# Reordering routing, setup and row gathers around the expert halves of a four-layer attention and mixture-of-experts kernel

## The chip, the core and the metric

The kernel runs on one core of one Trainium2 chip. The metric is the device time of one execution in microseconds. The engines are named as in the profile: PE (TensorE, matrix products), DVE (VectorE), ACT (ScalarE), POOL (GpSimd) and SP (SyncE, which here only issues transfers).

## The reference

Four layers run on `x`, 4 batches of 512 tokens with 128 channels, in float32. Each layer is a cross attention on a context of 154 rows per batch, added to `x`, and then a mixture of 8 experts, added to `x`. Both read a layer norm of `x`.

```python
x = x + _L0_xattn_ref(_layernorm(x), ctx, ...)      # bidirectional attention flow, one similarity
x = x + _L0_ffn_ref(_layernorm(x), ...)             # 8 experts, top 2, gated by silu
x = x + _L1_xattn_ref(ctx, ctx, _layernorm(x), ...) # 16 heads of 8, with a mask
x = x + _L1_ffn_ref(_layernorm(x), ...)             # 8 experts, top 1, capacity 321, gelu
x = x + _L2_xattn_ref(_layernorm(x), ctx, ...)      # 16 heads of 64, gated
x = x + _L2_ffn_ref(_layernorm(x), ...)             # 8 experts, top 2, gelu
x = x + _L3_xattn_ref(_layernorm(x), ctx, ctx, ...) # 16 heads of 64
x = x + _L3_ffn_ref(_layernorm(x), ...)             # 8 experts, top 2, relu
```

The reference computes every expert for every token and weighs the results; only the chosen experts have a weight that isn't zero.

## The kernel before

**Tiles and halves.** A batch is 4 tiles of 128 tokens (`NI`). All of `x` stays on the chip. The mixture is computed in two halves of two batches each: half 0 is batches 0 and 1, half 1 batches 2 and 3.

**Routing (`route`, L651).** A generator in steps: layer norm of the half's two batches (`stats` L218, whose power of -0.5 runs on POOL at L236; `norm` L239), transposes (`transposed` L248), logits (L666), the choice of experts (`top` L626), a rank of every token in its expert by products with a triangular matrix (L693, L695), and from it a row number in a buffer in HBM in which each expert owns whole blocks of 128 rows. One indirect transfer for each tile of 128 tokens and each choice scatters the normed rows there (`scatter` L721). The transfers are not issued at once: they are put in the list `rows_due`, and `row_transfers` (L641) issues the next few of them on POOL's queue, bound behind an instruction that it is given.

**Experts (`experts`, L825).** 23 blocks of 128 rows (15 where each token has one expert), in steps of one block (layer 0) or two. `load` (L835) fetches four blocks of tokens after all the scatters of the half, `tokens` (L846) transposes them (L850), `up` (L855) fetches the block's expert weights and multiplies (L877), and `down` (L882) applies the activation, multiplies with the second matrix (L916), copies the result to `ys` (L925, with `row_transfers` behind it) and stores it to `ybuf` in HBM (L928).

**Gather and combine (L948, L965).** After all stores of a half, each tile of tokens fetches its result rows by one indirect transfer per choice (L953) into `yg`, and DVE adds them with their weights to `x` (L971). `combine` requires that no row transfer is still due.

**Attention.** Layer 0 works on whole batches (`layer0_setup` L974). Layers 1 to 3 run a period for each tile of 128 tokens (`narrow_period` L435, `wide_period` L486), in which one tile's scores and exps (L308) run beside the previous tile's transposes of the probabilities (L371), their copies `pT` (L264, `take` L373, which issues two rows each) and products with the values (L408). The next batch is prepared in four parts, one for each tile (`at.parts`, for layer 1 at L1193). Before layer 1 to 3, batch 0 is prepared during the experts of the layer before, as `at.early` (mask, keys, values) and `at.late` (norm, its transpose, queries).

**Order.** In the attention of layers 1 to 3 the order on PE and ACT (in layers 2 and 3 on DVE too) is that of the program (`manual_schedule` L1305). Elsewhere, and on POOL, SP and layer 1's DVE, a scheduler with a model of times sets the order when the kernel is built: the program's order is the priority, and what it believes ready may go ahead. On the chip each engine then runs its instructions in that fixed order. The main loop (L1356 to L1399) sets the program's order: attention with half 0's routing inside, the next layer's setup, half 0's experts with half 1's routing inside, gather of half 0, early preparation, half 1's experts with the combining of half 0 inside, late preparation; half 1's rows are combined in the next layer's first periods.

## Time and profile before

| What | us |
|---|---|
| Median of 3 runs (1345.8 to 1351.96) | 1347.79 |
| The profiled execution's own time | 1282.47 |
| Its span, first to last instruction | 1280.8 |
| PE busy | 1089.4 |
| DVE busy | 731.6 |
| ACT busy | 565.3 |
| POOL busy | 253.6 |
| DVE waiting for gathered rows at L971, all of the kernel | 59.5 |

The profiled execution was shorter than the three timed runs. Its mean granted TensorE clock was 0.917 of full speed. The stages lie in its span about like this: layer 0's attention and first routing to 103 us, layer 0's experts to 262, layer 1's attention to 480, its experts to 573, layer 2's attention to 800, its experts to 906, layer 3's attention to 1140, its experts to 1251, and the last combining to the end.

A line of the order of time reads: start in us, duration in us, engine, line of the kernel, operation, output and inputs, count, and in brackets the idle time of the engine before it with what ended it. `PEld` is a weight load of TensorE, `issue` a time in which the engine waited for nothing that the profile shows. A line of the waits reads: engine and line that waited, what it waited for, us in total, number of times, longest.

### The profile page before, as it was taken

The page shows a single profiled execution, that of the slowest core. Times are in us where ns is not written, and L with a number is a line of the kernel's source. Part 1 is how long each engine was busy: PE and PEld are TensorE (multiplying, and loading weights), DVE is VectorE, ACT ScalarE, POOL GpSimd, SP SyncE. Part 2 cuts the span into 40 slices and gives each one's busy share as a digit, 9 for nine tenths or more (in the row PEclk, how much of TensorE's full clock was granted, in tenths as well). Part 3 has the DMA queues.
Part 4 walks back from the last instruction along what each step waited for, and adds up shares of the span by engine and source line. Part 5 has one row for each costly group of instructions (what it writes and reads, how often), then busy time and mean ns, then how long its engine had stood idle before and what let it go on. Part 6 is the DMA issues. An engine that isn't in the chain of part 4 may idle for free.

```text
span 1280.8 us, 26318 instructions
## 1 busy us (share of the span) xinstructions
PE 1089.4 (85%) x9351; PEld 896.9 (70%) x9351; DVE 731.6 (57%) x2012; ACT 565.3 (44%) x2264; POOL 253.6 (20%) x281
## 2 busy tenths in 40 slices
PE   4787998977878888889999998966899999899990
PEld 3657998933435448787878777855778788789890
DVE  6554646567666763335665776424476576646352
ACT  2113433454554543546656565321656665532230
POOL 2041315023000010232000004045220000402334
PEclk8767999988898988998999999887999999999996
DMA  7023786721100314433112214444421111334762
GB/s 228 1 81 113 216 253 189 207 94 25 23 19 26 100 38 119 133 110 84 35 35 55 64 37 123 123 150 133 127 55 45 41 35 35 109 95 143 209 191 60
DMA packets 136064, 126.77 MB, mean 99 GB/s; under 512 B 12538, under 2 KB 115583, under 8 KB 135551
## 3 DMA queue, kind: packets, MB, share of 16 engines
q1 hardware_dynamic: 128767, 110.39, 30.5%
q0 software_dynamic: 7168, 14.69, 3.9%
q8 instruction: 77, 1.26, 0.4%
q14 instruction: 52, 0.43, 0.1%
HBM read 101.31 MB, written 23.72 MB: 98 GB/s over the span
## 4 chain that ended last, share of the span: by engine, by line
PE 59%; DVE 12%; DMA 9%; issue 8%; ACT 5%; POOL 5%; SPq 2%; POOLq 0%; DVEq 0%
PE sc L877 11%; PE av L916 6%; PE tr L371 6%; PE sc L607 5%; PE av L408 5%; PE tr L425 5%; PE sc L592 3%; DMA yg<-ybuf,su 3%; POOL yg L953 3%; ACT probs L308 3%; DVE nm L294 3%; PE sc L1175 2%; DMA w<-in_up 2%; PE av L390 2%; PE tr L358 2%
## 5 line engine op out<-in xcount | busy, mean ns | idle before, releaser
L308 ACT ACTIVATE probs<-sc,nm 128x154 f32<-128x154 f32 x768 | 286.9, 403 | 162.7 <-DVE nm L294 162.5
L877 PE MATMUL sc<-tokT,w 128*128 128x128 f32 x1528 | 201.3, 286 | 8.7 <-DMA w<-in_up 3.6
L877 PEld LDWEIGHTS sc<-tokT,w 128*128 128x128 f32 x1528 | 189.0, 200 | 15.5 <-ACT eg L900 5.2
L294 DVE TENSOR_REDUCE nm<-sc 128x6 f32<-128x924 f32 x144 | 142.6, 1007 | 74.8 <-PE sc L607 49.1
L308 ACT ACTIVATION_READ_ACCUMULATOR probs<-sc,nm 128x1 f32 x768 | 168.3, 219 | 0.0
L916 PE MATMUL av<-w,hT 128*128 x1160 | 155.3, 279 | 3.2 <-DVE hT L905 2.5
L953 POOL DMA_INDIRECT yg<-ybuf,su x112 | 106.7, 952 | 246.5 <-ACT pT L267 59.9
L722 POOL DMA_INDIRECT buf<-xn,su x112 | 109.6, 979 | 227.0 <-DVE eb L745 97.3
L916 PEld LDWEIGHTS av<-w,hT 128*128 128x128 f32 x1160 | 141.9, 193 | 8.9 <-issue 4.7
L236 POOL TENSOR_TENSOR rstd<-ve,nhalf 128x4 f32<-128x4 f32 x32 | 33.0, 1032 | 547.3 <-DVE ve L234 429.6
L264 DVE COPY pT<-tr 128x512 f32<-128x512 f32 x160 | 106.9, 684 | 45.3 <-PE tr L371 41.5
L408 PE MATMUL av<-pT,vm 128*64 128x128 f32 (+1 forms) x1536 | 106.2, 284 | 22.5 <-DVE pT L264 22.4
L371 PE MATMUL tr<-ident,probs 128*128 128x128 f32 x768 | 123.1, 291 | 1.5 <-DVE rT L337 1.5
L371 PEld LDWEIGHTS tr<-ident,probs 128*128 128x128 f32 x768 | 86.1, 146 | 33.4 <-issue 21.7
L408 PEld LDWEIGHTS av<-pT,vm 128*64 128x64 f32 (+1 forms) x1536 | 63.8, 126 | 55.7 <-DVE pT L264 30.9
L900 ACT ACTIVATE eg<-sc,w 128x128 f32<-128x128 f32 x184 | 52.9, 368 | 89.5 <-PE sc L877 82.1
L607 PE MATMUL sc<-kT,qT 64*128 64x154 f32 x1024 | 87.1, 308 | 4.8 <-ACT probs L308 4.8
L905 DVE SCALAR_TENSOR_TENSOR hT<-sc,w,eg 128x128 f32<-128x128 f32 x184 | 56.2, 342 | 51.0 <-ACT eg L900 51.0
L607 PEld LDWEIGHTS sc<-kT,qT 64*128 64x128 f32 x1024 | 71.3, 189 | 15.8 <-issue 9.9
L592 PE MATMUL sc<-xnT,wq 128*128 128x128 f32 x512 | 73.6, 303 | 4.7 <-ACT probs L308 2.3
L592 PEld LDWEIGHTS sc<-xnT,wq 128*128 128x128 f32 x512 | 67.3, 212 | 10.2 <-issue 3.6
L425 PE MATMUL tr<-wo,aT 128*128 128x128 f32 x512 | 66.2, 284 | 1.6 <-DVE xnT L256 1.3
(255 smaller groups left out, 1432.2 us busy)
## 6 DMA issues: line engine op xcount, KB each, us to landing
w<-in_up SPq DMA_DIRECT2D x46, 516.0 KB
w<-in_up SPq DMA_DIRECT2D x76, 258.0 KB
rep<-rd SPq DMA_DIRECT2D x64, 256.0 KB
tok<-buf SPq DMA_DIRECT2D x36, 256.0 KB
ybuf<-ys SPq DMA_DIRECT2D x58, 128.0 KB
w<-in_down SPq DMA_DIRECT2D x3, 2048.0 KB
w<-in_up SPq DMA_DIRECT2D x46, 128.0 KB
ybuf<-ys SPq DMA_DIRECT2D x52, 64.0 KB
```

The costliest lines, as they stand in the source:

```text
L264: return nc.vector.tensor_copy(o, i)
L294: nc.vector.tensor_reduce(self.at.heads(self.nm, g, n), self.sc[g][:, :, 0 : n * S2].rearrange("p j (s k) -> p j s k", s=n), AX.X, ALU.max ...
L308: nc.scalar.activation(self.pr[:, h, :], self.sc[g][:, j, s * S2 : (s + 1) * S2], AF.Exp, bias=self.nm[:, h : h + 1], accum_out=self.rs[:, ...
L371: nc.tensor.transpose(q[:, t * P : (t + 1) * P], self.pr[:, h, 0:P], ident)
L408: nc.tensor.matmul(av[rows, cols], v, self.pT[n][:, t, :], start=False, stop=last)
L425: nc.tensor.matmul(o[:, 0:D], self.aT[:, c, :], self.at.wo[:, c, :], start=(c == 0), stop=(c == self.nb - 1))
L592: nc.tensor.matmul(sc[:, c // 4, c % 4 * P : (c % 4 + 1) * P], wq[:, c * P : (c + 1) * P], at.xnT[:, i * P : (i + 1) * P], start=True, sto ...
L607: nc.tensor.matmul(sc[:, j, s * S2 : (s + 1) * S2], at.qT[i][rows, c, :], at.kT[rows, c, :], start=True, stop=True)
L722: ins = nc.gpsimd.indirect_dma_start(out=buf[half], out_offset=bass.IndirectOffsetOnAxis(ap=su[:, t : t + 1], axis=0), in_=xns[t // NI][:, ...
L877: nc.tensor.matmul(dst, w[:, b, at : at + P], xT, start=True, stop=True)
L916: nc.tensor.matmul(y[:, b * D : (b + 1) * D], hT[:, fc, :], w2[:, bass.ds(es[b], 1), fc, :].rearrange("p o d -> p (o d)"), start=(fc == 0) ...
L953: ins = nc.gpsimd.indirect_dma_start(out=yg[:, t, :], out_offset=None, in_=ybuf[half], in_offset=bass.IndirectOffsetOnAxis(ap=su[:, t : t ...
```

## The change

Six things are edited, and the halves get a table `GROUPS` of batches in place of fixed arithmetic (the groups stay as they were, two batches in each half).

1. *Routing of layer 0 by batch.* In layer 0 `route` does norm, transposes and logits of one batch in one step, then of the other. `attend_first` runs batch 0's step before tile 1's attention, batch 1's after it, and the first steps of half 1's routing before and after batch 3's attention.
2. *Setup.* `layer1_setup` is called after half 0's experts of layer 0, no longer before them.
3. *Keys ahead.* Half 1's first token transposes are ordered behind the last product of the early preparation.
4. *Gathers.* `yg` is one tile for each batch and choice. Batch 0's rows are issued at once behind the last store, the rest three or four for each `down`. Combining of half 0 is put after 3 (layer 0) or 2 steps of half 1's experts, where it was after 9, 3, 5 and 5.
5. *Layer 1's first tiles.* Half 1's gathers are issued behind the exps of the very first tile too, and their combining starts one tile earlier.
6. *Layer 1's parts.* The norm moves to the third part, its transpose to the fourth, together with keys and queries. Several small tiles have one buffer instead of two or four.

```diff
         def exp(self, g):
...
-                    nc.scalar.activation(
+                    ins = nc.scalar.activation(
...
+            if self.at.dh < 64 and self.at.first and self.i == 0:
+                row_transfers(3, ins)
...
-            self.tails = p2.tile([self.rows, 4, P], F32, tag="tails", name="tails")
+            self.tails = p2.tile([self.rows, 4, P], F32, tag="tails", name="tails", bufs=1)
...
-        lg = rsm("lg", NH, E)
-        found = [stats(x[2 * half + k]) for k in range(B // 2)]
-        yield
-        xns = [norm(x[2 * half + k], found[k], rt) for k in range(B // 2)]
-        yield
-        xnTs = [transposed(xn) for xn in xns]
-        yield
-        for k, xnT in enumerate(xnTs):
...
+        for some in ([b] for b in batches) if layer == 0 else (batches,):
+            found = [stats(x[b]) for b in some]
+            if layer:
+                yield
+            new = [norm(x[b], f, rt) for b, f in zip(some, found)]
+            if layer:
+                yield
+            xnTs = [transposed(xn) for xn in new]
+            if layer:
+                yield
+            for xnT in xnTs:
+                q = ps_tr()
...
+            yield
...
-                nc.tensor.transpose(q[:, c * P : (c + 1) * P], tok[:, c, :], ident)
+                ins = nc.tensor.transpose(q[:, c * P : (c + 1) * P], tok[:, c, :], ident)
+                if g == 0:
+                    wait_for(ins, ahead, "they fill the wait for the tokens")
...
-                2 * n, nc.vector.tensor_copy(ys[:, 0:n], y[:, 0 : n * D].rearrange("p (b d) -> p b d", b=n))
+                2 + n, nc.vector.tensor_copy(ys[:, 0:n], y[:, 0 : n * D].rearrange("p (b d) -> p b d", b=n))
...
+    class Gathered:
...
+        def __init__(self, choices):
+            self.rows = [p2.tile([P, NI, D], F32, tag="yg", name="yg", bufs=6) for _ in range(choices)]
+            self.begun = 0
...
-        assert not rows_due
-        for (cw, _), yg in zip(routed[1], got):
-            nc.vector.scalar_tensor_tensor(xi, yg[:, t, :], cw[:, t : t + 1], xi, ALU.mult, ALU.add)
+        while got[k].begun < NI * len(routed[1]):
+            row_transfers(1)
+        for (cw, _), yg in zip(routed[1], got[k].rows):
+            nc.vector.scalar_tensor_tensor(xi, yg[:, i, :], cw[:, t : t + 1], xi, ALU.mult, ALU.add)
...
-            at.parts = ((masks,), (xn, values), (xnT,), (keys_queries,))
+            at.parts = ((masks,), (values,), (xn,), (xnT, keys_queries))
...
         tiles = [prepare(b, found[b]) for b in range(2)]
         tiles[0](0)
+        first, second = (Steps(route(layer, half, *gates[layer])) for half in range(2))
         tiles.append(prepare(2, found[2]))
+        first.step(1)
         tiles[1](0)
-        beside = Steps(route(layer, 0, *gates[layer])).step(3)
+        first.step(1)
         tiles.append(prepare(3, found[3]))
-        beside.step(5)
+        first.step(4)
         tiles[2](0)
-        beside.step(1)
+        first.step(1)
+        second.step(1)
         tiles[3](0)
-        return beside.finish()
+        return first.finish(), second.step(1)
...
-                    step = nothing if (b, i) in ((0, 0), (0, 1), (2, 0)) else beside.step
+                    step = nothing if (b, i) in ((0, 0), (2, 0)) or layer > 1 and (b, i) == (0, 1) else beside.step
...
         row_transfers()
-        if layer < 3:
+        if 0 < layer < 3:
             prepare = setups[layer + 1]()
...
         stores = first.finish()
         row_transfers()
-        got = gather(0, routed[0], stores)
+        got = gather(layer, 0, routed[0], stores)
+        row_transfers(NI * TOP[layer])
+        early = ()
         if layer < 3:
+            if layer == 0:
+                prepare = setups[1]()
             at = prepare(0, found)
-            for part in at.early:
-                part()
-        second = Steps(experts(layer, 1, routed[1], w2)).step((9, 3, 5, 5)[layer])
-        for k in range(B // 2):
+            early = [part() for part in at.early][-1:]
+        second = Steps(experts(layer, 1, routed[1], w2, early)).step((3, 2, 2, 2)[layer])
+        for k, b in enumerate(GROUPS[layer][0]):
             for i in range(NI):
-                combine(0, k, i, routed[0], got)
+                combine(layer, 0, k, i, routed[0], got)
```

The values function of each layer now returns its last product, for the third edit. Layer 0's `xn` pool has four buffers instead of three.

## The prediction, as it was put on record

> **What bounds the kernel now.** I read the busy shares first, then who TensorE waited for in each stage, then the order of time around the longest waits.
>
> ```profile
> span 1280.8 us, 26318 instructions
> PE 1089.4 (85%) x9351; PEld 896.9 (70%) x9351; DVE 731.6 (57%) x2012; ACT 565.3 (44%) x2264; POOL 253.6 (20%) x281
> ```
>
> TensorE (PE) is the busiest engine. A scheduling change can only win the time in which it waits, so I list its waits by stage (us in total, times, longest). First the start, 0 to 110 us (layer 0's attention and its first routing):
>
> ```profile
> PE tr L251 <- DVE xn L243: 7.9, 2, 4.4
> PE tr L850 <- DMA tok<-buf: 6.5, 1, 6.5
> PE tr L693 <- DVE sel L687: 5.5, 1, 5.5
> ```
>
> L251 waits for a normed batch, L693 (ranks) for the top-2 choice on VectorE (DVE), L850 for tokens scattered to HBM and read back. Then 805 to 915 us, where layer 2's experts pass from half 0 to half 1 and layer 3 is prepared:
>
> ```profile
> PE tr L850 <- DMA tok<-buf: 11.0, 2, 10.1
> PE tr L251 <- DVE xn L243: 11.0, 2, 10.2
> ```
>
> Two stops of 10 us. GpSimd's (POOL) order of time explains the second:
>
> ```profile
> 854.07 0.96 POOL L722 DMA_INDIRECT buf<-xn,su  x1 [0.30 <-issue]
> 867.16 0.98 POOL L953 DMA_INDIRECT yg<-ybuf,su  x1 [12.12 <-DVE ys L925]
> ...
> 885.98 0.94 POOL L953 DMA_INDIRECT yg<-ybuf,su  x1 [0.30 <-issue]
> 886.94 1.05 POOL L236 TENSOR_TENSOR rstd<-ve,nhalf 128x4 f32<-128x4 f32 x1
> ```
>
> The last scatter ends at 855.0. Then POOL idles 12.12 us, because the first gather is tied to a result copy `ys` of the next half, issues 16 gathers in 20 us, and only then makes batch 0's `rstd`. Its input stood ready much earlier:
>
> ```profile
> 880.97 0.21 DVE L234 TENSOR_SCALAR ve<-mv 128x4 f32<-128x4 f32 x1
> ```
>
> and TensorE, next in its order, stands still until 889.2:
>
> ```profile
> 889.22 0.48 PE L251 MATMUL tr<-ident,xn 128*128 128x128 f32 x1 [10.17 <-DVE xn L243]
> ```
>
> In layer 1's first four attention tiles (262 to 312) PE's waits are
>
> ```profile
> PE av L408 <- DVE pT L264: 6.2, 3, 2.9
> PE tr L358 <- DVE res L1189: 5.3, 2, 4.5
> ```
>
> and DVE's own longest there is for gathered rows:
>
> ```profile
> DVE x L971 <- DMA yg<-ybuf,su: 6.7, 9, 1.6
> ```
>
> The gathers run from 274.1, where POOL starts behind a pT copy, to 300.2, and DVE, which runs in order, stops for them.
>
> **What the Trainium skill says.** (1) Perfetto Trace Analysis, the timeline of the Tensor Engine Instruction: ACT, DVE and GPSIMD are strict FIFO. The trace agrees: `rstd` started at 886.94 though `ve` ended at 881.2, with five gathers between. (2) DMA: Bandwidth & Descriptors, Anatomy of one DMA: about 2.0 us fixed plus bytes/436e3, an estimate of 2.15 us for a 64 KB row transfer. The chain of waits shows 2.4 to 3.7 us for `yg`, up to 5.0 beside layer 3's weight loads; I use 2.5 to 3.6. (3) TensorE: Matmul & The Clock Gate, Part 1: after an idle window of about 3.4 us the array runs at half clock. The trace agrees: sixteen L592 matmuls right after the 10 us stop took 3.78 us, at 925.6 they took 2.05.
>
> **The change part by part** (profiled execution: 1282.47 us, of which 1280.8 are span).
>
> *A. Layer 0's routing by batch, setup moved.* Before, both batches' 16 logit matmuls (2.04 us at 61.15) follow tile 3's similarity matmuls (2.42 at 58.94). After, batch 0's eight are done during tile 1 and batch 1's stand ahead of those: 2.42 + 1.02 = 3.4 us earlier. DVE interleaves other work, so I take -3. The norming wait itself (4.4) stays. Batches 2 and 3 are routed before experts start: 8 transposes (1.04 at 113.9) and 16 logit matmuls (2.04) leave a full PE and go partly into the 6.5 us token wait; batch 3's `xn` ends at 104.4, so evacuation 0.69 and logits 1.0 delay the tokens by some 0.6. Net -2. Layer 1's setup leaves this stage: four transposes (1.1 us) and a 0.5 us wait for `wo_r`, about 2 us of DVE, five small SP loads. It returns at about 190 us, where PE is 95% busy, so only the wait is won. The moved loads have no inputs and may issue whenever SP is free (a layer 2 load landed at 30); if that cover is gone, half 1's tokens wait one landing, about 2 us. **Sum A: -5 (bounds -8 to -1).**
>
> *B. Layer 0, half 0 to half 1.* The first gather is already at 193.8, right at the end of half 0; issuing eight without pacing starts nothing earlier. DVE waits 9.0 us for rows at 195 to 224; combining moves from step 9 to step 3. **0 (-2 to +3).**
>
> *C. Layer 1's attention.* Gathers are tied to the exps of the first tile, so they may start before any pT copy; what is late next is the last store of ybuf, which the chain shows taking 7.12 us from 262.1. So they start at 269.3, not 274.1, and without pauses: 16 x 1.26 = 20 us, the last landing near 291 instead of 302.6. Combining starts one tile earlier too. I return half of DVE's 6.7: -3.4. Against it: `xnT` moves into the part with the query matmul. The matmul now waits for a 0.68 evacuation behind a pT copy of 0.69, less the key matmul 0.43 that covers it: 0.25 to 0.95, I take 0.8, for three batches +2.4; ACT's exps stand behind that query copy. **-1 (-8 to +6).**
>
> *D. Layer 1 to 2.* Four gathers (top 1) start when the stores land, about 534, against 544.4. PE's waits there are 1.11 (L251) and 1.80 (L592, `xnT` in a crowded DVE). **-2 (-4 to +1).**
>
> *E. Layer 2 to 3.* Scatters still end at 855.0; eight gathers follow until 865.1, landing by 867.8; two combines 0.7, stats 0.5, `ve` 0.2: ready at 869. Four gathers of batch 1, tied to the first `ys` (866.5), hold POOL to 871.6; `rstd` 1.0, first norm 0.4: PE can go on at 873.2. The late parts stand after 4 steps instead of 7, where PE arrives at 872 (step 4 at 868.05, then the down product of 870.72). The stop falls from 10.2 to about 1.3, and sixteen L592 run at full clock, -1.7: -10.6. If POOL's order puts the last four gathers ahead too, 5 us return. I take **-8 (-11 to -2).** Stop 1, 10.1 us for tokens, stays.
>
> *F. Contention.* The early gathers (8 x 64 KB) share the DMA engines with the token loads (2.8 to 3.2 us, engines 28% busy there): +0.3 in three layers, **+1 (0 to +2).**
>
> *At nothing:* keys ahead of the token transposes, since in layers 1 and 2 they stand there already (L556 at 528.4 and 844.1, L850 at 535.9 and 859.4); the added wait is PE for PE, and holds only what followed in order. Three scatters a block instead of two, since half 1's scatters end at 164 and its tokens are used from 187. One buffer for `tails`, `eq` and the small tiles, since their reader stands before the next writer on an ordered engine; uncovered it is a wait of 0.6 at a `tails` copy. The tail after 1251 (16 gathers, 20 us) is untouched.
>
> **Sum:** -5 + 0 - 1 - 2 - 8 + 1 = -15, so 1267.5 against 1282.5. The shown runs have a median of 1347.79, 1.051 times the profiled execution. I do not know where that share lies and scale: 1267.5 x 1.051 = **1332**.
>
> **The rivals.**
> *Washed out:* `rstd` stays behind all sixteen gathers (E -2.5), early rows only shift DVE's stops (C +2.5), A -3, D -1, F +1: -3, 1279.5, 1345 scaled. For it: DVE and POOL are fixed orders made beforehand, and DVE already stops nine times in C.
> *Slower:* combining now comes 1 to 6 steps sooner in the second half. If DVE's order puts eight combines ahead of the expert copies, it waits 8 x 1.26 + 2.5 = 12.6 us after the last store in each of the four layers. PE has two blocks of work before it needs a copy (two result buffers), 4.2 to 5.8 us, so it loses 7.6: +30 on my -15, 1297.5, 1364 scaled. It decides from (15 + 6.4)/4 = 5.4 us per layer on. For it: at 200.4 L916 waited 2.5 us for `hT` behind row waits. Against: rows land earlier now, and in layer 2 DVE is idle until tokens come.
> *More:* every part at its good end and the clock kept: -33, 1249.5, 1313 scaled.
> *It doesn't do what it says:* true of the keys alone, which I count at nothing.
>
> **How the numbers follow.** About 0.5% (6.7 us) is what a measurement here can tell. My case (1322 to 1341) 0.52, more 0.20, washed out 0.16, slower 0.12. So faster 0.72, same 0.16, slower 0.12. The range 1314 to 1347 leaves out the slower case and the outermost of the others; the likeliest case's own range is 1322 to 1341.
>
> **What would show it.** E: the first `yg` gather within 1 us of the last scatter, `rstd` 8 or 12 gathers later, L251's wait under 3 us. C: first gather near 269, last near 289, DVE's row wait under 4. A: L693 about 3 us earlier, and logit matmuls inside the token wait near 100. D: L251 and L592 without waits near 555. Wrong if L971's waits grow by more than the stops shrink, or if the token waits grow.

## The result, and the profile after

The changed kernel takes 1370.97 us (median; 1368.2 to 1373.3), the kernel before on the same chip 1349.63: a ratio of 1.016, 95% interval 1.0125 to 1.0195. The forecast was 1332 us, faster by 1.2%; the change is slower by 1.6%.

One fact has to come first, because no number below can be read without it. The prediction's trace of the kernel before spans 1280.8 us, its timed runs took 1346 to 1352, and the prediction scaled by 1.051 without knowing why. The chips are of two kinds. On one kind the kernel before takes 1280 to 1281 us in the median (two groups of runs), on the other 1348 to 1356 (four groups); the trace had been taken on the first, the times on the second. One thing that differs is shown further on: TensorE's signals (the semaphore increments that tell the other engines that a product is done) are held up beside row transfers. So I call them **prompt** and **holding** chips. A trace may only be compared with one of the same kind. The page of the changed kernel's first trace, on a holding chip:

```profile
span 1366.5 us, 26291 instructions
...
PE 1116.8 (82%) x9351; PEld 914.8 (67%) x9351; DVE 731.7 (54%) x2012; ACT 562.8 (41%) x2262; POOL 254.9 (19%) x281
```

and of the kernel before on a holding chip (experiment c1):

```profile
span 1344.9 us, 26318 instructions
...
PE 1112.0 (83%) x9351; PEld 913.4 (68%) x9351; DVE 728.7 (54%) x2012; ACT 563.9 (42%) x2264; POOL 253.6 (19%) x281
```

TensorE's busy time differs by 4.8 us of the 21.6, so it is mostly waiting that grew. To see where, I took marks from the timelines (first and last product of TokenT with the up weights in each half, first and last exp of an attention, last result copy) and the time between them, in us:

| stretch | prompt: before, after | holding: before, after | predicted |
|---|---|---|---|
| start to the first expert product | 108.2, 126.0: **+17.8** | 110.4, 126.8: **+16.4** | A, with the next: -5 |
| layer 0, half 0 | 74.4, 70.9: -3.5 | 75.7, 75.1: -0.6 | |
| layer 0, half 1 | 75.4, 75.3: -0.1 | 77.6, 86.3: **+8.7** | B: 0 |
| layer 1, first to last exp | 216.6, 215.7: -0.9 | 214.6, 217.7: +3.1 | C: -1 |
| layer 1's experts | 95.7, 94.1: -1.6 | 99.2, 95.6: -3.6 | D: -2 |
| layer 2's attention | 223.6, 224.3: +0.7 | 235.0, 237.4: +2.4 | |
| layer 2's experts | 108.6, 99.8: **-8.8** | 122.2, 110.5: **-11.7** | E: -8 |
| layer 3's attention | 230.9, 227.8: -3.1 | 247.5, 249.6: +2.1 | |
| layer 3, half 0 | 67.6, 70.1: +2.5 | 74.7, 74.5: -0.2 | |
| layer 3, half 1 | 46.3, 47.6: +1.3 | 55.7, 61.0: **+5.3** | |

On prompt chips the stretches of B, C, D and E moved about as forecast (C's by luck, as the last part shows), and A's did not. On holding chips two more stretches are lost, both beside gathers that are issued without a pause.

**The start.** TensorE's waits, 0 to 130 us, of the changed kernel on a prompt chip (us in total, times, longest):

```profile
PE tr L260 <- DVE xn L252: 21.6, 5, 5.1
```

L260 is the old L251, where the list of before had 7.9 in 2. One of those, 3.5 us, is the first norm of the kernel in both. The other, 4.4 before, has become four: 4.67, 4.45, 5.14 and 3.9, one for each batch. What one of them is made of stands in the timeline of all engines (start, us, engine, line, operation, and the idle time before it with its releaser):

```profile
89.15 0.39 PE L1119 MATMUL av<-wc,xnT 128*128 128x128 f32 x2
89.58 0.69 DVE L1122 TENSOR_TENSOR res<-av,bqv 128x512 f32<-128x512 f32 x1 [3.76 <-PE av L1119]
90.30 0.69 DVE L1124 TENSOR_TENSOR x<-x,res 128x512 f32<-128x512 f32 x1
...
91.03 0.87 DVE L236 BATCH_NORM_STATS2 st<-x 128x6 f32<-128x128 f32 x4
91.82 0.36 DVE L238 BATCH_NORM_AGGREGATE mv<-st 128x2 f32<-128x6 f32 x4
...
92.21 0.17 DVE L243 TENSOR_SCALAR ve<-mv 128x4 f32<-128x4 f32 x1
93.11 1.04 POOL L245 TENSOR_TENSOR rstd<-ve,nhalf 128x4 f32<-128x4 f32 x1
94.19 1.12 DVE L252 TENSOR_SCALAR xn<-x,mv,rstd 128x128 f32<-128x128 f32 x4 [1.81 <-POOL rstd L245]
94.68 1.15 PE L260 MATMUL tr<-ident,xn 128*128 128x128 f32 x4 [5.14 <-DVE xn L252]
```

A tile's last product ends at 89.5; residual, statistics, GpSimd's rstd (behind a row transfer) and norm follow one another, and TensorE does nothing, because the transposes of just this batch are next in its order. Only then comes the next tile:

```profile
96.62 1.88 PE L687 MATMUL tr<-wg,xnT 128*128 128x8 f32 x8 [0.78 <-DVE xnT L98]
98.35 1.09 PE L1074 MATMUL tr<-ident,sim 128*128 128x128 f32 x4
```

In the kernel before, the next tile's similarity (L1033) stood in the middle of the tile ahead of it:

```profile
33.27 1.20 PE L1078 MATMUL av<-wqv,ft 128*128 128x128 f32 x4
...
34.47 1.06 PE L1033 MATMUL tr<-ident,sim 128*128 128x128 f32 x4
...
61.15 2.04 PE L666 MATMUL tr<-wg,xnT 128*128 128x8 f32 x16
```

The last lines show a second price: the eight logit products of each batch took 1.88 us, sixteen before took 2.04, 0.235 us each against 0.128. The eight at 96.62 begin 1.9 us after their stop ends, the sixteen 3.7 us after theirs (the one of 4.4 us), with other products between. The Trainium skill, TensorE: Matmul & The Clock Gate, Part 1, has the array at half clock after an idle window of about 3.4 us; the trace agrees here, where each of the four stops is longer than that, but a shorter stop, 2.6 us in layer 2 to 3 below, did it too.

**Layer 2 to 3.** GpSimd's order of time on the prompt chip, around the last scatter:

```profile
865.51 0.96 POOL L744 DMA_INDIRECT buf<-xn,su  x1 [0.30 <-issue]
866.77 0.98 POOL L988 DMA_INDIRECT yg<-ybuf,su  x1 [0.30 <-issue]
...
882.75 0.95 POOL L988 DMA_INDIRECT yg<-ybuf,su  x1 [0.30 <-issue]
883.73 1.05 POOL L245 TENSOR_TENSOR rstd<-ve,nhalf 128x4 f32<-128x4 f32 x1
```

The first gather follows the last scatter at once (before: 12.12 us of idling), and rstd comes after 12 gathers instead of 16. TensorE's and VectorE's waits, 815 to 922:

```profile
DVE x L1012 <- DMA yg<-ybuf,su: 15.5, 10, 5.8
...
PE tr L875 <- DMA tok<-buf: 8.8, 1, 8.8
...
PE tr L260 <- DVE xn L252: 3.7, 3, 2.6
```

```profile
886.19 0.33 PE L260 MATMUL tr<-ident,xn 128*128 128x128 f32 x1 [2.59 <-DVE xn L252]
...
889.35 3.62 PE L604 MATMUL sc<-xnT,wq 128*128 128x128 f32 x16
```

The stop of 10.2 us is 2.6; the token wait stays, as predicted. VectorE waits longer for rows than before (9.6 us in 9 there). The sixteen query products behind the stop still take 3.62 us, about as slow as the 3.78 before, so the 1.7 us that E had for them at full clock did not come.

**Held signals.** On the holding chip, layer 0 half 1 has a stop that belongs to no instruction:

```profile
222.86 0.61 PE L943 MATMUL av<-w,hT 128*128 x4
...
228.70 0.95 POOL L988 DMA_INDIRECT yg<-ybuf,su  x1 [0.30 <-issue]
230.89 0.29 DVE L952 COPY ys<-av 128x128 f32<-128x128 f32 x1 [8.78 <-remote]
...
231.49 1.23 PE L943 MATMUL av<-w,hT 128*128 x4 [8.03 <-issue]
```

VectorE's copy waits for a TensorE product that ended at 220.1, and TensorE for what VectorE would do next. The trace also has the times at which TensorE's semaphore was counted up. Nine of its instructions that count it end in this stretch, and nine increments are recorded; set side by side in order:

```
instruction ends  218.34  218.86  219.61  220.08  223.02  223.25  223.47  232.29  232.72
increment         219.47  226.64  229.46  230.87  235.25  235.29  235.33  235.37  235.41
```

The fourth is the end of the product that the copy needs: 230.87, and the copy starts at 230.89. The fifth, 12.2 us late, is the up product that ScalarE needs, and ScalarE goes on at 235.27. So these two pairs are confirmed by the engines that waited; the first three are paired by order alone, and four increments just before them are missing from the record. The last five come in a burst 40 ns apart, 1.6 us after GpSimd's run of gathers ended (233.65). Counting as late an increment that is recorded more than 0.35 us from the end of every instruction making one:

| trace | TensorE late | of these in the 3 us after a row transfer's start | span, us |
|---|---|---|---|
| before, prompt | 2 of 1338 | 0 | 1280.8 |
| after, prompt (c2) | 2 of 1331 | 0 | 1283.7 |
| before, holding (c1) | 109 of 1305 | 98 | 1344.9 |
| after, holding | 89 of 1307 | 70 | 1366.5 |

The stretches of 3 us after a row transfer's start make up 26% of the span in c1 and hold 98 of its 109 late increments. Over all traces the two kinds stand apart: 72 to 109 late increments in each of eleven, 2 in each of nine. ScalarE's and VectorE's increments are not late on either kind (2 of 745 and 2 of 1761 in c1). On holding chips some increments are missing from the record (1305 of 1342 made), so the counts are lower bounds.

### The profile page after: what moved, and what is told of

Read it like the earlier page. It is cut to its first block, busy times and chain, and to the rows that moved or that the text cites. A ratio compares the mean times of both kernels' runs of the same rounds, so it can differ in the third digit from the quotient of the medians.

```text
span 1366.5 us, 26291 instructions
## 1 busy us (share of the span) xinstructions
PE 1116.8 (82%) x9351; PEld 914.8 (67%) x9351; DVE 731.7 (54%) x2012; ACT 562.8 (41%) x2262; POOL 254.9 (19%) x281
## 3 DMA queue, kind: packets, MB, share of 16 engines
q1 hardware_dynamic: 128767, 110.39, 28.6%
## 4 chain that ended last, share of the span: by engine, by line
PE 61%; DVE 14%; issue 9%; DMA 6%; ACT 4%; another core or an unknown queue 2%; POOL 2%; SPq 2%; POOLq 0%; DVEq 0%; ACTq 0%
PE sc L904 12%; PE av L943 9%; PE av L419 6%; PE tr L382 6%; PE sc L619 5%; PE tr L436 4%; DVE nm L303 3%; ACT probs L317 2%; PE sc L604 2%; PE sc L1217 2%; PE av L401 2%; PE tr L369 1%; PE tr L875 1%; DVE pT L273 1%
## 5 line engine op out<-in xcount | busy, mean ns | idle before, releaser
L904 PE MATMUL sc<-tokT,w 128*128 128x128 f32 x1528 | 206.0, 289 | 19.3 <-issue 11.6
L904 PEld LDWEIGHTS sc<-tokT,w 128*128 128x128 f32 x1528 | 193.6, 204 | 25.9 <-issue 16.4
L943 PE MATMUL av<-w,hT 128*128 x1160 | 162.6, 285 | 35.9 <-issue 32.3
L943 PEld LDWEIGHTS av<-w,hT 128*128 128x128 f32 x1160 | 146.6, 198 | 44.5 <-issue 37.0
L419 PE MATMUL av<-pT,vm 128*64 128x128 f32 (+1 forms) x1536 | 108.0, 285 | 25.9 <-DVE pT L273 24.0
L952 DVE COPY ys<-av 128x256 f32<-128x256 f32 (+1 forms) x110 | 38.9, 356 | 103.7 <-PE av L943 58.0
L436 PE MATMUL tr<-wo,aT 128*128 128x128 f32 x512 | 72.2, 301 | 2.4 <-DVE xnT L265 1.3
L604 PE MATMUL sc<-xnT,wq 128*128 128x128 f32 x512 | 70.9, 296 | 2.9 <-ACT probs L317 2.0
```

The costliest lines, as they stand in the source:

```text
L419: nc.tensor.matmul(av[rows, cols], v, self.pT[n][:, t, :], start=False, stop=last)
L436: nc.tensor.matmul(o[:, 0:D], self.aT[:, c, :], self.at.wo[:, c, :], start=(c == 0), stop=(c == self.nb - 1))
L604: nc.tensor.matmul(sc[:, c // 4, c % 4 * P : (c % 4 + 1) * P], wq[:, c * P : (c + 1) * P], at.xnT[:, i * P : (i + 1) * P], start=True, sto ...
L904: nc.tensor.matmul(dst, w[:, b, at : at + P], xT, start=True, stop=True)
L943: nc.tensor.matmul(y[:, b * D : (b + 1) * D], hT[:, fc, :], w2[:, bass.ds(es[b], 1), fc, :].rearrange("p o d -> p (o d)"), start=(fc == 0) ...
```

## The experiments

All times have the kernel before on the same chip beside them; the ratio to it is what is compared.

**c1: the kernel before, for a second trace.** No edit.

> The kernel before, unchanged, for a second trace of it: its profiled execution in the prediction (1282.5 us) is 65 us shorter than its timed runs (1346 to 1352), that of the changed kernel (1368.2) is not. Theory 'signals': in the trace after, TensorE's semaphore increments reach the waiting engines late, in bursts (89 of 1307 more than 0.35 us after the instruction that makes them; in the trace before 2 of 1338), and the five longest stops (8.8, 7.5, 11.7, 6.8, 8.4 us) are such ones. If that is a state of the machine that every run now has, this one's trace spans 1345 to 1350 and has 50 or more late increments, and the stages are to be compared with it, not with the trace of 1280.8. If lateness comes from the change (gathers issued without pauses), this trace has under 10 late ones, and its profiled time is near 1282 again or its 65 us lie elsewhere.

Measured: 1346.17, ratio 0.9998 (0.9969 to 1.0027), 109 late increments, span 1344.9. The lateness is there without the change; my first theory, that the change brings it, falls. The change can still bring more or fewer row transfers into its way.

**a1: gathers of half 0 paced as before**, on the changed kernel.

```diff
-        row_transfers(NI * TOP[layer])
-        second = Steps(experts(layer, 1, routed[1], w2, early)).step((3, 2, 2, 2)[layer])
+        second = Steps(experts(layer, 1, routed[1], w2, early)).step((9, 3, 5, 5)[layer])
...
-                2 + n, nc.vector...
+                2 * n, nc.vector...
```

> The changed kernel with the gathers of half 0 paced as before (none issued at once, two per block behind a result copy, combining after step 9, 3, 5, 5). Theory 'signals by unpaced gathers': the long stops of VectorE at the three changes of half go, 30 to 40 us, and the time is 1330 to 1342, below the kernel before. Theory 'start': the loss is layer 0's routing by batch, which this keeps; the time stays within 5 us of 1371. The prediction's own reasoning (gathers first are a gain of 8 at layer 2 to 3) expects 1379.

Measured: 1365.45, ratio 1.0157 (1.0078 to 1.0237), not told apart from the changed kernel's 1.016. That is the number of theory 'start', but not for its reason, and the other two expectations miss: two effects cancel. Against the changed kernel layer 0's half 1 falls from 86.3 to 76.1 and layer 3's from 61.0 to 53.6, while layer 2's experts rise from 110.5 to 121.8. So E's gain is real, and unpaced gathers cost at least as much elsewhere on this kind of chip. GpSimd's timeline in layer 0 shows the runs of four:

```profile
214.29 0.94 POOL L988 DMA_INDIRECT yg<-ybuf,su  x1 [0.30 <-issue]
218.17 0.94 POOL L988 DMA_INDIRECT yg<-ybuf,su  x1 [2.93 <-DVE hT L932]
...
221.92 1.06 POOL L988 DMA_INDIRECT yg<-ybuf,su  x1 [0.30 <-issue]
225.61 0.94 POOL L988 DMA_INDIRECT yg<-ybuf,su  x1 [2.63 <-DVE hT L932]
```

and TensorE's increments come in bursts of five at 216.1, 223.9, 231.3 and 238.7, each 0.5 to 1 us after the end of a run.

**a2: the start and layer 1's setup as before**, on the changed kernel: layer 0 routes two batches at once after tile 1, half 1 behind the first experts, and the setup of layer 1 stands ahead of the experts.

```diff
-        first, second = (Steps(route(layer, half, *gates[layer])) for half in range(2))
         tiles.append(prepare(2, found[2]))
-        first.step(1)
         tiles[1](0)
-        first.step(1)
+        first = Steps(route(layer, 0, *gates[layer])).step(3)
         tiles.append(prepare(3, found[3]))
-        first.step(4)
+        first.step(5)
         tiles[2](0)
         first.step(1)
-        second.step(1)
         tiles[3](0)
-        return first.finish(), second.step(1)
+        return first.finish(), Steps(route(layer, 1, *gates[layer]))
...
-        for some in ([b] for b in batches) if layer == 0 else (batches,):
+        for some in (batches,):
...
-        if 0 < layer < 3:
+        if layer < 3:
             prepare = setups[layer + 1]()
...
-            if layer == 0:
-                prepare = setups[1]()
```

> The changed kernel with layer 0's routing by two batches at once, half 1's routing behind the first experts and layer 1's setup ahead of the experts, all as before. Theory 'start': the first expert product is at 126.8 us in the trace after and at 108.2 before; undone, it is back at 108 to 112 and the time falls by 15 to 19, to 1353 to 1356. Theory 'signals by unpaced gathers': the start's 18 us are partly late signals too, so it falls by under 8. The prediction (a gain of 5 there) expects 1376.

Measured: 1354.93, ratio 1.0055 (1.0025 to 1.0085); the first expert product at 110.5. By this stretch the start is 16 of the 21 us that the change costs on this kind of chip, by the ratios 14. Without it the kernel is still slower than before here, by half a per cent.

**a3: layer 1's parts and gathers in the old order**, on the changed kernel.

```diff
-            at.parts = ((masks,), (values,), (xn,), (xnT, keys_queries))
+            at.parts = ((masks,), (xn, values), (xnT,), (keys_queries,))
...
-            if self.at.dh < 64 and self.at.first and self.i == 0:
-                row_transfers(3, ins)
```

> The changed kernel with layer 1's parts in the old order (keys and queries in the last part alone) and its gathers not tied to the first tile's exps. The prediction gave this part -1 (bounds -8 to +6), so undone 1372 (1365 to 1379). Both theories, 'signals' and 'start', expect 1371 within 4; if the 5.3 us stop of VectorE at a pT copy beside gathers at 311 comes of the exp-tied gathers, 1366.

Measured: 1364.07, ratio 1.0133 (1.0081 to 1.0185), which overlaps the changed kernel's. Its own stretch became longer (221.9 from first to last exp), so this says nothing of the part.

**a4: the routing put back, the setup left moved.** As a2, without its edit of the setup.

> The changed kernel with layer 0's routing put back (two batches at once, half 1 behind the first experts), but layer 1's setup left where the change put it. Undoing both gave 1354.9. Theory 'norms': the 16 us of the start are TensorE's stops for a batch just normed, so this is within 4 of 1355 and the first expert product is at 107 to 111. Theory 'setup': the moved setup (loads, four transposes beside the gathers) costs half 1 of layer 0 its 8 us more than before; then this is 1360 or more and the stretch from the last product of half 0 to that of half 1 is 84 to 87 us, with setup undone it was 86 as well, which speaks against it already.

Measured: 1365.14 where the kernel before took 1355.62: 1.0064 (1.0035 to 1.0092). The same as a2's 1.0055, so moving the setup costs or brings nothing that these intervals, some 4 us either way, can tell.

**a5: only batches 2 and 3 normed late**, on the changed kernel: `second` isn't stepped in the start.

> The changed kernel with batch 0 and 1 normed one by one as changed, but batches 2 and 3 normed behind the first experts, as before. In the trace after TensorE stops 4.7, 4.5, 5.2 and 3.9 us at L260, once for each batch; before it stopped once ahead of the experts, 4.4. Theory 'norms': the two stops for batches 2 and 3 and their products go from the start (9.1 us of stops, some 5 of transposes and logits with their evacuation waits); the first expert product comes at 114 to 119 instead of 126.8 and the time is 7 to 11 lower, about 1362. If the start is bound by something else (loads, scatters), the first expert product stays near 126.

Measured: 1.0147 (1.0102 to 1.0192), not the 7 to 11 us expected. The first product came 6 us earlier (120.7), and layer 0's half 0, which now has that routing, took 4.7 longer. But a stop of 10 us at TensorE that the changed kernel doesn't have lies in this start,

```profile
101.33 1.87 PE L1101 MATMUL av<-ebt,xn 128*128 128x1 f32 x8 [10.13 <-ACT ebt L1098]
```

while TensorE's increments of work ended by 91 are counted at 94.1, 96.2 and 100.5: held signals. They may hide as much as the two stops that were taken out, so this run does not tell which of the four batches carry the loss.

**m1 and m2: the parts that paid, together.** m1 is a2 with gathers first only in layers 1 and 2; m2 has also a3's edit.

```diff
-        row_transfers(NI * TOP[layer])
+        if layer in (1, 2):
+            row_transfers(NI * TOP[layer])
...
-        second = Steps(experts(layer, 1, routed[1], w2, early)).step((3, 2, 2, 2)[layer])
+        second = Steps(experts(layer, 1, routed[1], w2, early)).step((9, 2, 2, 5)[layer])
...
-                2 + n, nc.vector...
+                2 + n if layer else 2, nc.vector...
```

> The changed kernel with the start and the setup as before and the gathers of half 0 taken first only in layers 1 and 2; in layers 0 and 3 paced, with the old combining steps. From the stage times against the kernel before of the same chip: start 0, layer 0 half 1 about 0, layer 1 to 2 -4, layer 2 to 3 -11, layer 3 half 1 0, layer 1's attention +3: 1335 to 1338, 0.8 to 1% faster than before. Theory 'late signals': unpaced gathers cost in every layer; then layers 1 and 2 gain nothing either and it is 1346 or more.

> As the run before it, and layer 1's attention parts and gathers in the old order too. Undone on the changed kernel alone this gave 1364 against 1371 there, with intervals that overlap. If layer 1's new order costs the 3 us that its stage shows (217.7 from first to last exp, before 214.6), this is 3 faster than the run before it; the prediction (a gain of 1) has it 1 slower. Within 2 of it: no effect.

Measured on a holding chip: m1 0.9881 (0.9846 to 0.9915), m2 0.9826 (0.9788 to 0.9863). m1 gains slightly more than expected (1.2% where 0.8 to 1 was), and both beat both kernels. Layer 2's experts take 108.9 and 111.9 (122.2 before), layer 1's 93.1 and 93.9 (99.2), and the start is back at 108.0 and 110.3. The intervals of m1 and m2 overlap.

**a6 and c3: batch by batch, but one tile later.** The changed kernel with each batch's routing emitted behind the next tile.

```diff
         tiles.append(prepare(2, found[2]))
-        first.step(1)
         tiles[1](0)
-        first.step(1)
+        first.step(2)
         tiles.append(prepare(3, found[3]))
         first.step(4)
         tiles[2](0)
         first.step(1)
-        second.step(1)
         tiles[3](0)
+        second.step(1)
```

> The changed kernel, batches still normed one by one, but each batch's routing is emitted after the next tile instead of ahead of it (batch 0's norm and logits after tile 1, batch 2's after tile 3). Theory 'norms': in the changed kernel TensorE's order runs tile, norm, tile, norm, so it stands still at L260 once per batch with nothing else in its queue; one tile later batch 0's norm is long ready and tile 1 fills tile 0's gaps. The stops at L260 ahead of the experts fall from four (18.2 us) to two or three, the first expert product from 126.8 to 112 to 117, the time by 8 to 13, to 1358 to 1363 where the changed kernel has 1371. If the split into single batches itself costs (eight small norms, two logit evacuations), the first expert product stays above 122.

> The changed kernel with each batch's routing emitted after the next tile, a second time. Theory 'norms': 10 to 16 us below the changed kernel in the same call, whichever kind of chip; the first expert product near 110. If the gain was of that chip: within 4 of the changed kernel.

Measured: these fell on prompt chips, where a6 is 0.9959 (0.9932 to 0.9986) and c3 0.9972 (0.9951 to 0.9994), c3 13 us below the changed kernel beside it (1273.5 against 1286.4). TensorE's waits in c3, 0 to 130 us, and its order of time:

```profile
PE tr L260 <- DVE xn L252: 7.3, 2, 3.8
```

```profile
34.89 1.06 PE L1074 MATMUL tr<-ident,sim 128*128 128x128 f32 x4
...
54.28 0.96 PE L687 MATMUL tr<-wg,xnT 128*128 128x8 f32 x8
...
59.07 1.15 PE L260 MATMUL tr<-ident,xn 128*128 128x128 f32 x4 [3.83 <-DVE xn L252]
```

The next tile's similarity is back inside the tile ahead of it (34.89), batch 0's eight logits take 0.96 instead of 1.88 us, and two stops are left of five. The busy times up to the first expert product settle it (length, then TensorE's busy time and matmuls). The kernel before:

```profile
0.00:108.20 108.20, 71.02 (x326) 55.12 (x326) 62.18 (x253) 16.67 (x55) 29.25 (x49) 0.74 0.32 98
```

the changed kernel, c2:

```profile
0.00:126.00 126.00, 82.28 (x346) 63.02 (x346) 63.15 (x252) 17.21 (x56) 29.60 (x49) 0.70 0.27 84
```

one tile later, c3:

```profile
0.00:108.60 108.60, 78.75 (x347) 62.12 (x347) 62.00 (x252) 17.28 (x56) 29.01 (x49) 0.70 0.32 97
```

c2 and c3 have the same matmuls but for one, and 43.7 us of idling against 29.9: 13.8 of the 17.4 us between them are idling, the rest slower matmuls. Splitting into batches costs nothing; where each is put in TensorE's order does. Against the kernel before, the +17.8 of c2 are 6.5 of idling and 11.3 of busy TensorE, since half 1's routing came into the start, with twenty matmuls more in all and its logits at the slow clock. That idling grew by only 6.5 although the stops at L260 grew by 13.7 has a reason that the text on A needs: the waits for the ranks (5.5) and for the tokens (6.5) are gone in c2. c3 lacks them too, so it idles 7.3 us less than the kernel before.

**c2 and c4: the changed kernel and m2 on a prompt chip.** No edits.

> The changed kernel, unchanged. On a chip that holds signals (about 100 late increments, kernel before near 1350): 1.016 again. On one that doesn't (2 late, kernel before near 1281): theory 'start' keeps the 16 us there, since no increment before 147 us was late in the first trace; layer 0 half 1 costs 2.4 instead of 9, layer 2 to 3 gains 8.7: 1288 to 1292, 1.006 to 1.009. If held signals were the cause of the start too, it is below 1280 there, as the prediction had it (1267.5).

> Start, setup and layer 1's attention as before, gathers first in layers 1 and 2 only, a second time. On a chip that holds signals 0.983 again. On one that doesn't: layer 1 to 2 -3, layer 2 to 3 -8, the rest 0: 1270, 0.991.

Measured: c2 1286.43 against 1279.85, a ratio of 1.0074 (1.0043 to 1.0106), the ratio that the theory of the start gave (1.006 to 1.009); the first expert product at 126.0. c4 1269.13, 0.992 (0.9893 to 0.9948). So the loss at the start is there on both kinds, with none of its signals held, and the rest of the 1.6% belongs to holding chips.

**p1, c5 and c6: fewer row transfers at a time.** m2 with half 0's gathers in layers 0 and 3 at half the rate, and batch 1 combined later.

```diff
-                2 + n if layer else 2, nc.vector...
+                n if half and layer in (0, 3) else 2 + n if layer else 2, nc.vector...
...
-            second.step(2 // PER[layer])
+            second.step((8, 1, 1, 4)[layer])
```

> The best version so far (0.983 of before) with the gathers of half 0 in layers 0 and 3 issued at half the rate: one a block in layer 0 instead of two, two a pair of blocks in layer 3 instead of four, and batch 1 combined later to suit. Theory 'run length': TensorE's signals are held as long as GpSimd issues row transfers one after another and get through when the run ends (in the paced run at 216.1, 223.9, 231.3, 238.7, each 0.5 to 0.9 us after four transfers in a row). Runs of one or two then hold them 1.3 to 2.6 us at most; layer 0's second half takes 74 to 76 us instead of 76.8, layer 3's 46 to 49 instead of 51.3, and the time is 3 to 6 lower. If what counts is the number of row transfers, both stretches stay within 1 us and the time within 3.

> The best version with the gathers of half 0 at half the rate in layers 0 and 3, a second time. Theory 'run length', where signals are held: 3 to 6 us below the best version in the same call, from layer 0's second half (74 to 76 us against 76.8) and layer 3's (46 to 49 against 51.3). Where they are not held: within 2 of it. If the number of transfers counts: within 2 on both kinds.

> The best version with the gathers of half 0 at half the rate in layers 0 and 3, a third time, hoping for a chip that holds signals (kernel before near 1350). Theory 'run length' there: 0.978 to 0.981 against 0.983 for the best version, layer 0's second half 74 to 76 us (best 76.8), layer 3's 46 to 49 (best 51.3). Theory 'number of transfers': 0.983, both stretches within 1 us. Where signals are not held: 0.991 again.

Measured: on prompt chips 0.9917 (0.9888 to 0.9945) and 0.991 (0.987 to 0.9951), as m2. On a holding chip (c6) 0.9797 (0.9743 to 0.9851), the lowest ratio of all, though its interval overlaps m2's. Layer 3's half 1 is clear: it takes 46.2 us (m2 51.3), as much as the kernel before takes on a prompt chip (46.3). Layer 0's half 1 has no late increment (m2 24) and takes 74.5 us (m2 76.8), but 2.1 of this are given back before layer 1's first exp, and prompt chips show the same step, so there nothing is won. Over all traces, in us:

| row transfers beside the experts | layer 0, half 1: prompt; holding | layer 3, half 1: prompt; holding |
|---|---|---|
| eight without a pause (three traces; five) | 75.3 to 77.8; 85.3 to 86.3 | 47.6 to 49.7; 60.6 to 61.2 |
| two a block, in layer 3 four a pair (four; five) | 74.9 to 76.5; 76.1 to 77.8 | 46.1 to 47.3; 51.3 to 55.7 |
| half of that (p1 and c5; c6) | 73.2 to 73.8; 74.5 | 48.6 to 49.7; 46.2 |

The denser row transfers are issued, the more a holding chip takes over a prompt one; between the last two rows this shows in layer 3 alone. Their number is the same in all rows. In the traces of holding chips the runs without a pause are 12 to 16 long in the first row (the eight, and those that follow at once), two to four in layer 0 and four to eight in layer 3 in the second, one in layer 0 and two in layer 3 in the third. The rows also differ in the steps at which results are combined, but that is so on prompt chips too, where they lie close together. How many increments are late doesn't give the loss (in layer 0's half 1 24 in m2, 8 in the changed kernel).

**m3, m4 and c7: layer 1's attention in parts.** m2 with only the new parts (m3, c7), or only the gathers tied to exps (m4).

> The best version so far (0.983 of before) with layer 1's attention parts in the new order (values, norm, then transposes and queries in one part), gathers in the old order. The prediction put +2.4 on this part alone (three batches by 0.8). From the stages of nine kernels the new parts and the new gathers together cost layer 1's attention 4.9 us (223.0 from first to last exp against 218.1). If the parts are the cause: 3 to 6 slower; if the gathers are: within 2.

> The best version so far (0.983 of before) with layer 1's gathers tied to the first tile's exps as changed, parts in the old order. The prediction put -3.4 on it. Theory 'run length': 16 gathers in nine or so behind ACT come as one long run in layer 1's first tile, and TensorE's signals are held there: 1 to 4 slower, with a stop of 4 us or more between 275 and 300. If earlier gathers pay as predicted: 3 faster.

> The best version with layer 1's new attention parts and the old gather order, a second time. Where signals are held: from the stage times of nine kernels (223.0 us with new parts and gathers, 218.1 with neither) 0.983 to 0.987. If the parts are a gain of 3 there as on the other kind: 0.979 to 0.981. Where signals are not held: 0.987 again.

Measured on a prompt chip: m3 0.9868 (0.9834 to 0.9901), m4 0.9916 (0.9883 to 0.9948), beside m2's 0.992 elsewhere; on a holding chip c7 0.9854 (0.9809 to 0.9899). c7 lies where the theory of a cost had it, but its interval overlaps m2's, and its stretch (218.4) is within 1 us of m2's. The new parts may gain on a prompt chip (213.7 us from first to last exp, before 216.6), but other kernels' stretches there scatter from 215.7 to 220.5, so I leave it at "no loss shown". The gathers tied to exps bring nothing to be measured (m4).

## Why the prediction was wrong

**A failed, and is the largest part.** Predicted -5 for the start, measured +17.8 and then -3.5 in half 0, so +14.3 on a prompt chip. There it decides the sign: +2.9 with it, some -11 without it, by an estimate from the stretches. On the holding chip it does not do so alone: with the start undone (a2) the ratio is still 1.0055, because of B below. The step was "The norming wait itself (4.4) stays", with "Net -2" for batches 2 and 3. I moved the instructions one by one (8 transposes, 16 logits) and never asked what TensorE has in its order between a tile's last product and its batch's transposes. Before, that was the next tile, and one wait of 4.4 was left for two batches; after, nothing, four times, 18.2 us. The ranks came 7.4 us later (76.11 against 68.67) instead of about 3 earlier. What A hoped for was there: the waits for ranks and tokens went, 12.0 us together, and one tile later (c3) they go without the stops. The prediction had even read that TensorE is an ordered engine at E, and didn't use it here. It also took the logits at full clock, 1.02 for eight; after a stop they took 1.88.

**B** (0) was the second step to fail, on holding chips alone: -0.1 on a prompt chip, as predicted, but +8.7 on a holding one, and +5.3 in layer 3's half 1, for which only F's contention stood, by signals held through gathers without a pause. "Issuing eight without pacing starts nothing earlier" was true, but not that it costs nothing. m1, which undoes the start and these two, is faster than before (0.9881).

**C** (-1): -0.9 on a prompt chip, by luck: a6 and c3, with the same layer 1, take 220.3 and 220.5 us there, where the kernel before takes 216.6. The first gather comes 8.5 us after the first exp (12.4 before) and the last 28.6 (38.4 before), as worked out; but VectorE's row wait did not fall from 6.7 to under 4, it rose to 8.1 us. The +2.4 for the query product was not found (m3, c7). On holding chips +3.1, within the scatter of that stretch. So whether C gains or loses stays open.

**D** (-2): -1.6 and -3.6. **E** (-8): -8.8 and -11.7, by the mechanism given: gather at once after the scatter, rstd after 12 gathers, a stop of 2.6 instead of 10.2. Undone in a1, the stretch came back to 121.8 us. Its clock term alone failed: the query products stayed slow, as shown above.

**F** (+1): layer 3's halves rose by 2.5 and 1.3 on a prompt chip, but prompt traces of that last stretch scatter from 46.1 to 49.7. Layer 3's attention is 2 to 3 us shorter in all prompt traces with any of the change (227.5 to 228.9, before 230.9); no run takes that apart.

**The scaling** by 1.051 was no scaling at all: it joined a trace from one kind of chip to times from the other. The sum against its own trace was -15; with A as measured (+14.3 for -5) it would have been +4, and the trace says +2.9 (the medians on a prompt chip 6.6).

**The rivals.** "Slower" named combines ahead of expert copies, in each layer's second half, each losing 7.6 us. On a prompt chip (c2) those stretches moved by -0.1 to +1.3 in layers 0 and 3 and the experts of 1 and 2 shrank, so that mechanism did not act there. On holding chips the +8.7 and +5.3 of layers 0 and 3 are near its size, but by held signals. "Washed out" had E at -2.5 and A at -3: neither.

**Open.** Why some chips hold TensorE's increments, and what in a row transfer does it, no run shows; only when (beside row transfers), for whom (TensorE alone) and that density matters. Nor does any run show what makes up most of the level between the two kinds, some 50 us of which stand in the best-paced kernel too (1321.0 in c6 against 1270.5 in c5). Of the four chips whose numbers are on record, 10 and 13 were holding and 7 and 11 prompt, and only chip 10 was used at two times (holding at both), so whether a chip keeps its kind is hardly shown. The kernel that norms one tile later (a6, c3) was not timed on a holding chip.

## What to carry to other kernels

Before splitting or moving a step, write down what the in-order engine has queued between the step's input and its use: if that is only the step itself, the whole chain of other engines (here 3.9 to 5.1 us a time) is idle time for it, however little the step costs. Emit a dependent step one unit of independent work later. And compare a trace only with times from a machine of the same level: when a profiled execution and the timed runs differ by 5%, settle that first, and pace row transfers where signals turn out to wait for them.

## What was not expected of the hardware

- TensorE's semaphore increments can be held while GpSimd issues indirect row transfers (0.95 us each and 0.30 between): 12.2 us in the case shown, released in bursts about 40 ns apart after the run, a few singly within it. 72 to 109 a trace are late on some chips, 2 on others; ScalarE's and VectorE's are not (2 of 745 and 2 of 1761 in c1).
- The kernel before takes 1280 us on the one kind and 1350 on the other; between two traces of it the longer stretches are layer 2's attention (+11.4), its experts (+13.6), layer 3's attention (+16.6) and its experts (+16.5), all of them with row transfers beside TensorE. But layer 1's attention has them too and is not longer (-2.0). Not all of it need be held signals: TensorE's busy time also rose from 1089.4 to 1112.0, and its mean granted clock is 0.905 where it was 0.917; whether as a cause or because of the stops, no run shows.
